# A tuned four-layer kernel: normalizing the early gates during the recurrence instead of in the gate stage

## The chip, the cores and the metric

The kernel runs on one core of one Trainium2 chip. The metric is the device time of one execution in microseconds (us). Several executions are timed and the median is given. One further execution is taken with the hardware profiler; every duration of a single instruction below comes from that one.

## The reference, cut to what matters

The input x has 16 sequences of 512 steps of 512 features. Four layers follow each other, each added to x. The change touches the third (L2) and the fourth (L3); the second (L1) sets the order in which everything can start.

```python
x = x + L0(x)                        # here: a gate per sequence and feature
# L1, a recurrence over the 512 steps
h = tanh(x_t @ Wx + b + h @ Wh);     x_t = x_t + h
# L2, over whole sequences, column by column of 512 features
f = sigmoid(x @ Wf.T + bf);  i = sigmoid(x @ Wi.T + bi);  c = x @ Wc.T + bc
s = f + i + 1e-8;  F = f / s;  I = i / s * c
scaling = exp(suffix sums of log(F + 1e-8))          # here: a product scan from the end
hidden  = cumsum(scaling * I) + exp(cumsum(log(F + 1e-8))) * h0
x = x + hidden
# L3, a matrix per sequence: base + low rank (rank 8), made from cond
layer = base + A_b @ B_b.T;          x = x + x @ layer
```

F and I of a step depend on that step alone, so they can be made as soon as L1 has finished the step. The scans need the whole sequence.

## The kernel before, in words

The program has two stages.

**The recurrence** (lines 399 to 478) goes through 64 blocks `n` of 8 steps `s`. Its instructions on TensorE, ScalarE, VectorE and SyncE stand in the order in which the source writes them (line 400). In each step TensorE does 16 matmuls of h with Wh (`accumulate`, L337, 32 instructions in the trace, since a matmul of this type is two instructions there), 8 matmuls of x with Wx for the next block (`inputs`, L337 too), and in part of the steps something else. ScalarE then does four tanh (L446) and VectorE four 32-wide transposes (L447), which give the h that the next step's matmuls wait for. After the transposes VectorE does one more operation in each step: the addition that makes L2's input x2 (L454, in steps 4 to 7 of a block, since the steps are added in pairs), or the gating of a later block's x (`gated`, L163, in steps 0 to 3).

Blocks 1 to 16 also make the low-rank factors of L3, in steps 4 to 7 of each block (`factor_part`, L309), in a PSUM bank with the tag `pf`.

**Early gates.** The weights of L2 are used on the first TE = 128 steps of every sequence already during the recurrence (`early_gate`, L379). One piece `q` is one k-chunk of one unit: 4 matmuls with 256 columns (2 sequences of 128 steps), put at the end of a recurrence step, while TensorE would otherwise wait for tanh and transposes. Four pieces make a unit: one of the three gates, for one of four 128-feature chunks `j`, for a pair of sequences. There are 8 pairs x 12 units x 4 = 384 pieces. They begin in block N_GATES = 17, one per step, and the last block does two per step. ScalarE takes each finished unit out of PSUM (`keep_gate`, L392: a sigmoid for f and i, the bias alone for the candidate), and SyncE's queue stores it in a DRAM tensor `early` with three parts (L393). Units alternate between two PSUM banks, `pf` and `pg`.

**The gate stage** (lines 481 to 589) goes through the 16 sequences `b`, and for each through 4 units `j` (`gate_unit`). A unit is 3 x 4 matmuls with the remaining 384 columns (L495) into `pf`, `pi` (one PSUM bank each) and `pc` (two banks), two sigmoids on ScalarE (L511), three loads of the early parts on SyncE's queue (L508 and L510), and eleven operations on VectorE: f + i + EPS (L512), the reciprocal of it (L513), f times it (L514), EPS added (L515), i times it (L516), i times the early candidate (L517, 128 columns), i times the new candidate straight from PSUM (L518), and three scans and a product (L522, L525, L526, L528). GpSimd adds the two parts (L531) and x2 (L532), which gives x3, L3's input. The tiles f, i and s have two buffers each, so a unit's sigmoid waits until GpSimd is done with the unit two before.

`make_layer` makes L3's matrix for sequence b after its unit j = 2: four matmuls (L553) into PSUM (`pl`, two in banks of its own and two in the banks of `po`), four copies on ScalarE (L559), and four additions of the base matrix on GpSimd (L560). For the last sequence VectorE adds into the base matrix itself (L557). `last_layer` of sequence b - 1 is done after unit j = 1 of sequence b: 16 matmuls with 512 columns (L567), evacuations on ScalarE (L571) and stores (L572). For the last sequence, b = 15, that `last_layer` of sequence 14 comes after j = 3, and its own follows as the last work of the program. In this stage a scheduler sets the order of each engine's instructions.

Of the kernel before, what the change touches and what calls it, by code (L numbers as in the profile page):

```python
# [30 lines left out]
F32 = mybir.dt.float32  # L31
# [4 lines left out]
P = 128  # L36
# [15 lines left out]


TE = 128
N_GATES = TE // T + 1
EPS = 1e-8
LN_EPS = 1e-5

# [5 lines left out]
def kernel(  # L64
# [27 lines left out]
    def col(which, j):  # L92
        return vec_sb[:, which * KC + j : which * KC + j + 1]
# [13 lines left out]
    base_sb = keep.tile([P, KC, D], F32)  # L107

    dram = ctx.enter_context(tc.tile_pool(name="dram", bufs=1, space=bass.MemoryType.DRAM))
    early = dram.tile([B, 3, KC, P, TE], F32, name="early")  # L110
    factor = [dram.tile([B, R, D], F32, name=f"factor_{i}") for i in range(2)]

    rnn = ExitStack()
# [253 lines left out]

    def early_gate(q):

        unit, k = divmod(q, KC)  # L370
        b, unit = divmod(unit, 3 * KC)
        which, j = divmod(unit, KC)
        pair = slice(2 * b, 2 * b + 2)
        if k == 0:
            pool, tag = ((ps_p, "pf"), (ps_q, "pg"))[unit % 2]
            early_gate.ps = pool.tile([P, 2, TE], F32, tag=tag, name=f"pg_{b}_{unit}")
        w = (wf_sb, wi_sb, wc_sb)[which]
        for c in range(KC):
            nc.tensor.matmul(  # L379
                early_gate.ps[c * BP : (c + 1) * BP, :, :],  # L380
                w[:, k, j * P + c * BP : j * P + (c + 1) * BP],
                x2[:, k, pair, :TE],
                start=(k == 0),
                stop=(k == KC - 1),
                skip_group_check=True,
            )
        return (pair, which, j, early_gate.ps) if k == KC - 1 else None

    def keep_gate(pair, which, j, ps):
        got = w2pool.tile([P, 2, TE], F32, tag="gate", name=f"gate_{pair.start}_{which}_{j}")  # L390
        func = AF.Identity if which == 2 else AF.Sigmoid
        nc.scalar.activation(got, ps, func, bias=col((C_BF, C_BI, C_BH)[which], j))  # L392
        nc.sync.dma_start(out=early[pair, which, j].rearrange("b p t -> p b t"), in_=got)  # L393

    def fresh(n):
        return [ps_r.tile([P, G, P], F32, tag=f"pre{i}", name=f"pre_{n}_{i}") for i in range(NBANK)]
# [8 lines left out]
    for n in range(NBLK):  # L405
        if n + 1 < NBLK:
            nxt = fresh(n + 1)
        if n + 2 < NBLK:
            xs.append(new_x1(n + 2))
        if n == 0:  # L410
            loaded = load_first()
        coming = None
        for s in range(T):
            odd = s % 2
            g = next(i for i, pair in enumerate(PAIRS) if s in pair)
            for k in range(KC):
# [12 lines left out]
            if loaded and s >= KC:  # L429
                factor_part(loaded, s - KC, *((straight, hT3) if n else (tile_columns, aeT)))  # L430
            made = []
            if n >= N_GATES:
                q = (n - N_GATES) * T + s
                qs = (q,) if n + 1 < NBLK else (q + s, q + s + 1)
                made = [gate for gate in map(early_gate, qs) if gate]
            a = apool.tile([P, P], F32, tag="a", name=f"a_{n}_{s}")

            h = h_out[s]
            if odd:
                turned, h_prev = h[:, :, :BP], h[:, :, B:]  # L440
            else:
                turned, h_prev = h[:, :, B:], h[:, :, :BP]
            bank, place = PLACE[g]
            for c in range(KC):
                at = slice(c * BP, (c + 1) * BP)
                nc.scalar.activation(a[:, at], pre[bank][:, place, at], AF.Tanh)  # L446
                nc.vector.transpose(turned[:, c, :], a[:, at])  # L447
            for gate in made:
                keep_gate(*gate)
            if s == max(PAIRS[g]):  # L450
                t0, t1 = PAIRS[g]
                step = t1 - t0
                at = slice(n * T + t0, n * T + t1 + step // abs(step), step)
                nc.vector.tensor_tensor(  # L454
                    x2[:, :, :, at].rearrange("p k b t -> p k t b"),
                    xs[n][:, :, t0 // 2, :, :],
                    turned.rearrange("p k (t b) -> p k t b", t=2),
                    ALU.add,
                )
# [30 lines left out]
    def gate_unit(b, j, x3):  # L490
        ps = []
        for w_sb, tag, bufs in ((wf_sb, "pf", 1), (wi_sb, "pi", 1), (wc_sb, "pc", 2)):
            p = ps_g.tile([P, S], F32, tag=tag, name=f"{tag}_{b}_{j}", bufs=bufs)
            for k in range(KC):
                nc.tensor.matmul(  # L495
                    p[:, TE:],
                    w_sb[:, k, j * P : (j + 1) * P],
                    x2[:, k, b, TE:],
                    start=(k == 0),
                    stop=(k == KC - 1),  # L500
                )
            ps.append(p)
        pf, pi, pc = ps
        f = work.tile([P, S], F32, tag="f", name=f"f_{b}_{j}")
        i = work.tile([P, S], F32, tag="i", name=f"i_{b}_{j}")
        s = work.tile([P, S], F32, tag="s", name=f"s_{b}_{j}")
        c = work.tile([P, TE], F32, tag="c", name=f"c_{b}_{j}")
        nc.sync.dma_start(out=c, in_=early[b, 2, j])  # L508
        for which, (gate, p, bias) in enumerate(((f, pf, C_BF), (i, pi, C_BI))):
            nc.sync.dma_start(out=gate[:, :TE], in_=early[b, which, j])  # L510
            nc.scalar.activation(gate[:, TE:], p[:, TE:], AF.Sigmoid, bias=col(bias, j))  # L511
        nc.vector.scalar_tensor_tensor(s, f, EPS, i, ALU.add, ALU.add)  # L512
        nc.vector.reciprocal(s, s)  # L513
# [4 lines left out]
        nc.vector.scalar_tensor_tensor(  # L518
            i[:, TE:], pc[:, TE:], col(C_BH, j), i[:, TE:], ALU.add, ALU.mult
        )  # L520
# [11 lines left out]
        nc.gpsimd.tensor_tensor(x3[:, j, :], s, x2[:, j, b, :], ALU.add)  # L532
# [13 lines left out]
    def make_layer(b, at, bt, layer):  # L546
# [6 lines left out]
            nc.tensor.matmul(pl, at[rows, :], bt[rows, :], start=True, stop=True)  # L553
            made.append(pl)
        for c, pl in enumerate(made):
            if layer is base_sb:
                nc.vector.tensor_tensor(layer[:, c, :], pl, layer[:, c, :], ALU.add)  # L557
# [90 lines left out]
```

## Time and profile before

| | us |
|---|---|
| median of 3 runs | 1698.56 |
| lowest and highest of them | 1697.42, 1702.98 |
| the profiled execution | 1701.3 |
| its span, first to last instruction | 1699.5 |
| TensorE busy | 1643.3 (97%) |
| VectorE busy | 1152.2 (68%) |
| ScalarE busy | 428.3 (25%) |
| GpSimd busy | 311.1 (18%) |
| recurrence ends, first matmul of the gate stage | 925.3 |
| last matmul of the gate stage issued and evacuated | 1696 |

The engines are PE (TensorE's matmuls; PEld are its weight loads), DVE (VectorE), ACT (ScalarE), POOL (GpSimd) and SP (SyncE). Times in the timeline are counted from the first instruction. A line of the timeline gives the start, the time taken, the engine, the source line, the operation, its output and inputs, and how many instructions were merged into it; in brackets stands the idle time before it and what ended that. A line of the groups gives the busy time and the mean duration in ns, then the idle time of the engine before such instructions. A line of the windows gives a stretch of time, then busy time and instruction count by engine, the granted TensorE clock, the busy share of the DMA engines and GB/s.

### The profile page before, as it was taken

How to read it: one execution, taken by the hardware profiler on the slowest of the kernel's cores; microseconds unless marked ns; L12 is line 12 of the kernel's file. 1: busy time of each engine (PE TensorE's matmuls, PEld its weight loads, DVE VectorE, ACT ScalarE, POOL GpSimd, SP SyncE). 2: the span in 40 equal slices, each digit the busy share in tenths (PEclk: the TensorE clock that was granted, in tenths of full speed). 3: DMA queues.
4: the chain of work that ended last, by engine and by line, in shares of the span. 5: the costliest groups of instructions: out<-in, count | busy, mean ns of one | idle time of the engine just before them, and what ended most of it. 6: DMA issues, size and time to landing. Idle time of an engine off the chain costs nothing.

```text
span 1699.5 us, 71490 instructions
## 1 busy us (share of the span) xinstructions
PE 1643.3 (97%) x31205; PEld 1197.7 (70%) x31205; DVE 1152.2 (68%) x3305; ACT 428.3 (25%) x2407; POOL 311.1 (18%) x283
## 2 busy tenths in 40 slices
PE   5999999999999999999999889999999999999987
PEld 5888888998999989998997445555555555555543
DVE  3444544444444444444443989999999999999994
ACT  2222223333333333333333111111121112212111
POOL 2000000000000000000000433334444444434331
PEclk9999999999999999999999999999999999999998
DMA  5344331111111111111111011011111111111101
GB/s 190 102 147 152 109 93 39 42 42 42 36 46 41 42 38 39 45 42 39 42 41 36 16 41 45 30 45 38 38 44 44 44 44 44 43 45 44 46 19 50
DMA packets 118160, 92.01 MB, mean 54 GB/s; under 512 B 11843, under 2 KB 96323, under 8 KB 117846
## 3 DMA queue, kind: packets, MB, share of 16 engines
q1 hardware_dynamic: 117312, 87.42, 16.8%
q8 instruction: 244, 4.00, 1.0%
q14 instruction: 70, 0.57, 0.1%
q10 hardware_dynamic: 534, 0.02, 0.0%
HBM read 57.51 MB, written 29.88 MB: 51 GB/s over the span
## 4 chain that ended last, share of the span: by engine, by line
PE 90%; DVE 6%; issue 1%; ACT 1%; DMA 1%; POOL 1%; DVEq 0%; ACTq 0%; POOLq 0%
PE pre L337 39%; PE po L567 13%; PE pg L379 10%; PE pf L495 9%; PE pi L495 8%; PE pc L495 8%; DVE s L513 2%; PE pf L309 1%; PE pl L553 1%; PE pre L355 1%; DVE h_out L447 1%; ACT a L446 1%; DVE s L522 1%; DVE s L526 1%; DMA b2a_raw<-in_b2a_dram 0%
## 5 line engine op out<-in xcount | busy, mean ns | idle before, releaser
L447 DVE STREAM_TRANSPOSE h_out<-a 128x32 f32<-128x32 f32 x2048 | 264.7, 186 | 454.5 <-ACT a L446 453.4
L337 PE MATMUL pre<-wh_sb,h_out 128*32 128x128 f32 x16384 | 560.4, 274 | 7.7 <-DVE h_out L447 1.4
L337 PEld LDWEIGHTS pre<-wh_sb,h_out 128*32 128x32 f32 x16384 | 460.8, 110 | 97.0 <-DVE h_out L447 71.9
L446 ACT ACTIVATE a<-pre 128x32 f32<-128x32 f32 x2048 | 238.3, 202 | 581.8 <-PE pre L337 581.7
L337 PE MATMUL pre<-wx_sb,x 128*32 128x128 f32 x8192 | 334.2, 273 | 2.4 <-issue 1.7
L337 PEld LDWEIGHTS pre<-wx_sb,x 128*32 128x32 f32 x8192 | 242.5, 110 | 5.0 <-issue 4.0
L567 PE MATMUL po<-layer,x 128*128 128x512 f32 x480 | 213.9, 604 | 14.2 <-DVE base_sb L557 9.8
L513 DVE RECIPROCAL s<-s 128x512 f32<-128x512 f32 x64 | 214.0, 3344 | 1.5
L495 PE MATMUL pf<-x,wf_sb 128*128 128x384 f32 x512 | 180.8, 497 | 11.4 <-ACT f L511 10.8
L567 PEld LDWEIGHTS po<-layer,x 128*128 128x128 f32 x480 | 93.0, 194 | 129.6 <-issue 106.5
L495 PE MATMUL pi<-x,wi_sb 128*128 128x384 f32 x512 | 175.8, 486 | 0.0
L495 PE MATMUL pc<-x,wc_sb 128*128 128x384 f32 x512 | 175.6, 486 | 0.0
L531 POOL TENSOR_TENSOR s<-s,f 128x512 f32<-128x512 f32 x64 | 93.7, 1464 | 429.0 <-DVE s L526 173.9
L484 POOL MEMSET zero<- 128x1 f32 x1 | 0.1, 99 | 911.6 <-DMA early<-gate 911.6
L495 PEld LDWEIGHTS pf<-x,wf_sb 128*128 128x128 f32 x512 | 96.9, 192 | 92.9 <-issue 19.9
L495 PEld LDWEIGHTS pi<-x,wi_sb 128*128 128x128 f32 x512 | 97.6, 191 | 68.3 <-issue 0.8
L495 PEld LDWEIGHTS pc<-x,wc_sb 128*128 128x128 f32 x512 | 97.3, 190 | 67.8
L454 DVE TENSOR_TENSOR x<-x,h_out 128x128 f32<-128x128 f32 x256 | 101.0, 395 | 34.9 <-PE pg L379 11.7
L511 ACT ACTIVATE f<-pf,vec_sb 128x384 f32<-128x384 f32 x64 | 37.3, 582 | 300.6 <-POOL s L531 279.9
L571 ACT COPY osb<-po 128x512 f32<-128x512 f32 x64 | 37.5, 586 | 233.4 <-DMA out_dram<-osb 125.2
L560 POOL TENSOR_TENSOR layer<-layer,base_sb 128x512 f32<-128x512 f32 x60 | 90.9, 1544 | 11.0 <-ACT layer L559 11.0
L379 PE MATMUL pg<-x,wf_sb 128*32 128x256 f32 x1024 | 84.6, 379 | 0.0
(84 smaller groups left out, 1334.2 us busy)
## 6 DMA issues: line engine op xcount, KB each, us to landing
xb<-in_xT_dram SPq DMA_DIRECT2D x64, 256.0 KB
w<-in_l3w_dram SPq DMA_DIRECT2D x64, 256.0 KB
out_dram<-osb SPq DMA_DIRECT2D x64, 256.0 KB
early<-gate SPq DMA_DIRECT2D x96, 128.0 KB
c<-early SPq DMA_DIRECT2D x64, 64.0 KB
f<-early SPq DMA_DIRECT2D x64, 64.0 KB
i<-early SPq DMA_DIRECT2D x64, 64.0 KB
w_sb<-in_w1T_dram SPq DMA_DIRECT2D x1, 1024.0 KB
```

The costliest lines, as they stand in the source:

```text
L337: nc.tensor.matmul(pre[PLACE[g][0]][j * BP : (j + 1) * BP, PLACE[g][1], :], lhsT, tile_columns(w, j), start=False, stop=False, skip_group_ ...
L379: nc.tensor.matmul(early_gate.ps[c * BP : (c + 1) * BP, :, :], w[:, k, j * P + c * BP : j * P + (c + 1) * BP], x2[:, k, pair, :TE], start= ...
L446: nc.scalar.activation(a[:, at], pre[bank][:, place, at], AF.Tanh)
L447: nc.vector.transpose(turned[:, c, :], a[:, at])
L454: nc.vector.tensor_tensor(x2[:, :, :, at].rearrange("p k b t -> p k t b"), xs[n][:, :, t0 // 2, :, :], turned.rearrange("p k (t b) -> p k ...
L495: nc.tensor.matmul(p[:, TE:], w_sb[:, k, j * P : (j + 1) * P], x2[:, k, b, TE:], start=(k == 0), stop=(k == KC - 1),)
L511: nc.scalar.activation(gate[:, TE:], p[:, TE:], AF.Sigmoid, bias=col(bias, j))
L513: nc.vector.reciprocal(s, s)
L531: nc.gpsimd.tensor_tensor(s, s, f, ALU.add)
L560: nc.gpsimd.tensor_tensor(layer[:, c, :], layer[:, c, :], base_sb[:, c, :], ALU.add)
L567: nc.tensor.matmul(po, x3[:, k, at], layer[:, k, :], start=(k == 0), stop=(k == KC - 1))
L571: nc.scalar.copy(osb, po)
```

## The change

The early gates are now normalized during the recurrence, and only the two finished tiles F and I (without the EPS that is added to F) are stored in `early`.

- `early_gate(q)` begins with step 128, that is in block 16, and there is one piece in every step to the last, so the doubled pieces of the last block are gone. The order of the units is changed, so that f, i and candidate of one (pair, j) follow each other: 12 pieces are a group.
- What was `keep_gate` becomes a list of jobs, each filed under the step in which it is to be issued (`later`, `do_jobs`). `do_jobs` stands at the end of a step, after its transposes and its addition or gating. Counted in steps from the group's first piece: sigmoid of f at 5, sigmoid of i at 7 (ScalarE); the sum f + i + EPS at 8; the reciprocal in four pieces of 64 columns at 9, 10, 11 and 12; f times it at 13, with the store; i times it at 14; and i times the candidate, straight from PSUM, at 15, with the store. So VectorE gets one job in eight of twelve steps. The tiles come from the pool of the L3 weights (`w2`, 6 buffers). Jobs left over after the last step are issued there.
- `gate_unit` does the sum, the reciprocal and both products on the 384 new columns alone. The loads of the early candidate (L508) and the product L517 are gone; the two other loads stay. The addition of EPS (L515), the scans and the products with them still take all 512 columns.
- `make_layer` adds the base matrix on VectorE, straight from PSUM, for every sequence; the ScalarE copies and the GpSimd additions are gone.

```diff
-N_GATES = TE // T + 1
...
-    early = dram.tile([B, 3, KC, P, TE], F32, name="early")
+    early = dram.tile([B, 2, KC, P, TE], F32, name="early")
...
     def early_gate(q):
-        unit, k = divmod(q, KC)
-        b, unit = divmod(unit, 3 * KC)
-        which, j = divmod(unit, KC)
+        u, k = divmod(q, KC)
+        group, which = divmod(u, 3)
+        b, j = divmod(group, KC)
...
-            pool, tag = ((ps_p, "pf"), (ps_q, "pg"))[unit % 2]
+            pool, tag = ((ps_p, "pf"), (ps_q, "pg"))[u % 2 if u else 1]
...
-    def keep_gate(pair, which, j, ps):
-        got = w2pool.tile([P, 2, TE], F32, tag="gate", name=f"gate_{pair.start}_{which}_{j}")
-        func = AF.Identity if which == 2 else AF.Sigmoid
-        nc.scalar.activation(got, ps, func, bias=col((C_BF, C_BI, C_BH)[which], j))
-        nc.sync.dma_start(out=early[pair, which, j].rearrange("b p t -> p b t"), in_=got)
...
+        def part_of_reciprocal(at):
+            nc.vector.reciprocal(flat[:, at], flat[:, at])
+        def normalize_f():
+            nc.vector.tensor_tensor(f, f, s, ALU.mult)
+            store(0, f)
+        def times_candidate():
+            nc.vector.scalar_tensor_tensor(i, ps, col(C_BH, j), i, ALU.add, ALU.mult)
+            store(1, i)
+        if which == 0:
+            later(q if u == 0 else q + 2, lambda: sigmoid(f, C_BF))
+        elif which == 1:
+            later(q, lambda: sigmoid(i, C_BI))
+            later(q + 1, lambda: nc.vector.scalar_tensor_tensor(s, f, EPS, i, ALU.add, ALU.add))
+            for n in range(4):
+                at = slice(n * TE // 2, (n + 1) * TE // 2)
+                later(q + 2 + n, lambda at=at: part_of_reciprocal(at))
+            later(q + 6, normalize_f)
+            later(q + 7, lambda: nc.vector.tensor_tensor(i, i, s, ALU.mult))
+        else:
+            later(q + 4, times_candidate)
+    jobs = {}
+    def later(q, job):
+        jobs.setdefault(q, []).append(job)
+    def do_jobs(q):
+        for job in jobs.pop(q, ()):
+            job()
...
-            made = []
-            if n >= N_GATES:
-                q = (n - N_GATES) * T + s
-                qs = (q,) if n + 1 < NBLK else (q + s, q + s + 1)
-                made = [gate for gate in map(early_gate, qs) if gate]
+            q = n * T + s - TE
+            if q >= 0:
+                early_gate(q)
...
-            for gate in made:
-                keep_gate(*gate)
...
+            do_jobs(q)
...
+    for q in sorted(jobs):
+        do_jobs(q)
     rnn.close()
...
-        c = work.tile([P, TE], F32, tag="c", name=f"c_{b}_{j}")
-        nc.sync.dma_start(out=c, in_=early[b, 2, j])
+        old, new = slice(0, TE), slice(TE, S)
...
-        nc.vector.scalar_tensor_tensor(s, f, EPS, i, ALU.add, ALU.add)
-        nc.vector.reciprocal(s, s)
-        nc.vector.tensor_tensor(f, f, s, ALU.mult)
+        nc.vector.scalar_tensor_tensor(s[:, new], f[:, new], EPS, i[:, new], ALU.add, ALU.add)
+        nc.vector.reciprocal(s[:, new], s[:, new])
+        nc.vector.tensor_tensor(f[:, new], f[:, new], s[:, new], ALU.mult)
         nc.vector.tensor_scalar(f, f, EPS, None, ALU.add)
-        nc.vector.tensor_tensor(i, i, s, ALU.mult)
-        nc.vector.tensor_tensor(i[:, :TE], i[:, :TE], c, ALU.mult)
+        nc.vector.tensor_tensor(i[:, new], i[:, new], s[:, new], ALU.mult)
...
-            if layer is base_sb:
-                nc.vector.tensor_tensor(layer[:, c, :], pl, layer[:, c, :], ALU.add)
-            else:
-                nc.scalar.copy(layer[:, c, :], pl)
-                nc.gpsimd.tensor_tensor(layer[:, c, :], layer[:, c, :], base_sb[:, c, :], ALU.add)
+            nc.vector.tensor_tensor(layer[:, c, :], pl, base_sb[:, c, :], ALU.add)
```

More of the change, by code (lines that the diff above doesn't have):

```diff
@@ L368, in early_gate @@
     def early_gate(q):
-        unit, k = divmod(q, KC)
-        b, unit = divmod(unit, 3 * KC)
-        which, j = divmod(unit, KC)
+        u, k = divmod(q, KC)
+        group, which = divmod(u, 3)
+        b, j = divmod(group, KC)
         pair = slice(2 * b, 2 * b + 2)
         if k == 0:
-            pool, tag = ((ps_p, "pf"), (ps_q, "pg"))[unit % 2]
-            early_gate.ps = pool.tile([P, 2, TE], F32, tag=tag, name=f"pg_{b}_{unit}")
+            pool, tag = ((ps_p, "pf"), (ps_q, "pg"))[u % 2 if u else 1]
+            early_gate.ps = pool.tile([P, 2, TE], F32, tag=tag, name=f"pg_{u}")
+        ps = early_gate.ps
         w = (wf_sb, wi_sb, wc_sb)[which]
@@ L379, in early_gate @@
             nc.tensor.matmul(
-                early_gate.ps[c * BP : (c + 1) * BP, :, :],
+                ps[c * BP : (c + 1) * BP, :, :],
                 w[:, k, j * P + c * BP : j * P + (c + 1) * BP],
@@ L386, in early_gate, with store, sigmoid @@
             )
-        return (pair, which, j, early_gate.ps) if k == KC - 1 else None
-    def keep_gate(pair, which, j, ps):
-        got = w2pool.tile([P, 2, TE], F32, tag="gate", name=f"gate_{pair.start}_{which}_{j}")
-        func = AF.Identity if which == 2 else AF.Sigmoid
-        nc.scalar.activation(got, ps, func, bias=col((C_BF, C_BI, C_BH)[which], j))
-        nc.sync.dma_start(out=early[pair, which, j].rearrange("b p t -> p b t"), in_=got)
+        if q % (3 * KC) == 0:
+            early_gate.tiles = [
+                w2pool.tile([P, D], F32, tag="w2", name=f"{name}_{group}", bufs=6)[:, : 2 * TE].rearrange(
+                    "p (b t) -> p b t", b=2
+                )
+                for name in ("ef", "ei", "es")
+            ]
+        if k < KC - 1:
+            return
+        f, i, s = early_gate.tiles
+        flat = s.rearrange("p b t -> p (b t)")
+        def store(which, got):
+            nc.sync.dma_start(out=early[pair, which, j].rearrange("b p t -> p b t"), in_=got)
+        def sigmoid(gate, bias):
+            nc.scalar.activation(gate, ps, AF.Sigmoid, bias=col(bias, j))
+        def part_of_reciprocal(at):
[24 more added lines that the diff above has]
+            job()
     def fresh(n):
@@ L506, in gate_unit @@
         s = work.tile([P, S], F32, tag="s", name=f"s_{b}_{j}")
-        c = work.tile([P, TE], F32, tag="c", name=f"c_{b}_{j}")
-        nc.sync.dma_start(out=c, in_=early[b, 2, j])
+        old, new = slice(0, TE), slice(TE, S)
         for which, (gate, p, bias) in enumerate(((f, pf, C_BF), (i, pi, C_BI))):
-            nc.sync.dma_start(out=gate[:, :TE], in_=early[b, which, j])
-            nc.scalar.activation(gate[:, TE:], p[:, TE:], AF.Sigmoid, bias=col(bias, j))
-        nc.vector.scalar_tensor_tensor(s, f, EPS, i, ALU.add, ALU.add)
-        nc.vector.reciprocal(s, s)
-        nc.vector.tensor_tensor(f, f, s, ALU.mult)
+            nc.sync.dma_start(out=gate[:, old], in_=early[b, which, j])
+            nc.scalar.activation(gate[:, new], p[:, new], AF.Sigmoid, bias=col(bias, j))
+        nc.vector.scalar_tensor_tensor(s[:, new], f[:, new], EPS, i[:, new], ALU.add, ALU.add)
+        nc.vector.reciprocal(s[:, new], s[:, new])
+        nc.vector.tensor_tensor(f[:, new], f[:, new], s[:, new], ALU.mult)
         nc.vector.tensor_scalar(f, f, EPS, None, ALU.add)
-        nc.vector.tensor_tensor(i, i, s, ALU.mult)
-        nc.vector.tensor_tensor(i[:, :TE], i[:, :TE], c, ALU.mult)
+        nc.vector.tensor_tensor(i[:, new], i[:, new], s[:, new], ALU.mult)
         nc.vector.scalar_tensor_tensor(
-            i[:, TE:], pc[:, TE:], col(C_BH, j), i[:, TE:], ALU.add, ALU.mult
+            i[:, new], pc[:, new], col(C_BH, j), i[:, new], ALU.add, ALU.mult
         )
```

## The prediction, as put on record before the changed kernel ran

> **What bounds the kernel now.** I read the windows first. Their columns are the stretch, its length, busy us and instructions of PE, PEld, DVE, ACT and POOL, the granted clock, the DMA share and GB/s.
>
> ```profile
> 930.00:1000.00 70.00, 57.69 (x162) 30.72 (x161) 64.26 (x59) 9.28 (x17) 23.71 (x21) 0.93 0.10 29
> 1100.00:1300.00 200.00, 200.00 (x600) 107.18 (x599) 198.52 (x189) 39.69 (x73) 86.25 (x71) 1.00 0.13 43
> 1600.00:1650.00 50.00, 47.10 (x148) 25.89 (x148) 49.62 (x51) 8.61 (x16) 19.84 (x17) 0.97 0.12 40
> 1650.00:1699.50 49.50, 36.10 (x81) 16.17 (x79) 26.58 (x30) 5.74 (x10) 7.92 (x6) 0.88 0.12 47
> ```
>
> In the middle of the gate stage PE and DVE are both full, so the shares don't say which sets the pace. The timeline of PE does:
>
> ```profile
> 951.68 2.85 PE L495 MATMUL pf<-x,wf_sb 128*128 128x384 f32 x8 [1.81 <-ACT f L511]
> 964.07 4.54 PE L495 MATMUL pf<-x,wf_sb 128*128 128x384 f32 x8 [4.37 <-ACT f L511]
> 990.47 9.88 PE L567 MATMUL po<-layer,x 128*128 128x512 f32 x17 [4.43 <-POOL x L532]
> ...
> 1166.42 2.74 PE L495 MATMUL pf<-x,wf_sb 128*128 128x384 f32 x8
> 1169.00 2.74 PE L495 MATMUL pi<-x,wi_sb 128*128 128x384 f32 x8
> 1171.58 2.74 PE L495 MATMUL pc<-x,wc_sb 128*128 128x384 f32 x8
> 1174.16 13.90 PE L567 MATMUL po<-layer,x 128*128 128x512 f32 x32
> ...
> 1635.23 2.85 PE L495 MATMUL pf<-x,wf_sb 128*128 128x384 f32 x8 [1.30 <-ACT f L511]
> 1645.91 4.35 PE L495 MATMUL pf<-x,wf_sb 128*128 128x384 f32 x8 [1.60 <-ACT f L511]
> 1665.42 16.75 PE L567 MATMUL po<-layer,x 128*128 128x512 f32 x32 [9.81 <-DVE base_sb L557]
> ```
>
> From 1004 to 1632 no PE line has a bracket: each group of 8 starts 2.58 us after the last (7.74 us a unit), the 32 of L567 take 13.74, and every sequence takes the same 45.96 us. So the middle is bound by PE's streaming; DVE's 45.6 us a sequence just fit. DVE binds only at the two ends. Start: streaming alone would bring sequence 2's first pf at 925.34 + 6 units (46.44) + L553's slot (1.25) + 13.74 = 986.8; it starts at 1004.05, so 17.3 us are lost. End: from 1601.55, 6 units, two L553 slots (2.3) and twice 13.74 would end at 1677.8; the last matmul ends near 1695.8, so 18.0 are lost.
>
> The recurrence, by DVE's timeline (ACT's tanh ends the .71 of idle time):
>
> ```profile
> 894.33 0.49 DVE L447 STREAM_TRANSPOSE h_out<-a 128x32 f32<-128x32 f32 x4 [0.71 <-ACT a L446]
> 895.03 0.40 DVE L454 TENSOR_TENSOR x<-x,h_out 128x128 f32<-128x128 f32 x1 [0.20 <-PE pg L379]
> 896.13 0.49 DVE L447 STREAM_TRANSPOSE h_out<-a 128x32 f32<-128x32 f32 x4 [0.71 <-ACT a L446]
> ```
>
> A step with an early gate takes 1.74 us or a little more, all of it PE issue: .87 for Wh, .44 for Wx, .43 for the gate. Steps without one take 1.645 (blocks 1 to 16); there PE waits for h. So the h chain has .095 us of slack under PE in a gate step, and DVE is free from 895.43 to 896.13.
>
> [...] L515 takes .42 alone and 1.48 at 951.49, beside L560. [...] behind 4.37 and 9.81 us of idleness the groups at 964.07 and 1665.42 take 1.8 and 2.85 us more; behind 1.60 it happened too (1645.91), behind 1.81 it didn't.
>
> **Part 1: a gate unit on DVE.** In the timeline L512 starts at 1208.33 and again at 1219.12: 10.79 us a unit away from L560. Rows used:
>
> ```profile
> L513 DVE RECIPROCAL s<-s 128x512 f32<-128x512 f32 x64 | 214.0, 3344 | 1.5
> L204 DVE RECIPROCAL rstd<-std 16x1 f32<-16x1 f32 x1 | 0.1, 150 | 2.1 <-ACT std L202 2.1
> L557 DVE TENSOR_TENSOR base_sb<-pl,base_sb 128x512 f32<-128x512 f32 x4 | 2.6, 660 | 0.0
> ```
>
> The reciprocal costs (3344 - 150) / 511 = 6.25 ns a column, so 128 columns less save .80. L512, L514 and L516 lose 128 columns at 1.04 ns (L516 .68 at 512 columns, L517 .28 at 128): .13 each, .40. L517 goes, .20 start to start, and .26 that L516 lay blocked in that unit. 10.79 - .80 - .40 - .20 - .26 = 9.13 us. Added: four base additions a sequence, some .60 each: 2.4 (for b = 15 they were there). [...] DVE's sequence falls from 45.6 to 4 x 9.13 + 2.4 = 38.9 us. In the middle that is worth nothing: 45.96 is PE's. ACT's copies and SP's 64 loads of c are off the path as well. GpSimd's L531 and L532 (2.6 us) begin as DVE starts the next unit's L512 and reciprocal, which they didn't slow at 1208.33; I take the same.
>
> **Part 2: the start.** Left-over jobs: one reciprocal piece (.47), two products (.42 each by the slope) and the candidate (.48) behind the last L454, 1.6 to 1.7 us. The first pf waited for the last reader of the early PSUM (ACT, 925.35); now that is DVE, so PE starts at 926.9. The last store lands some 2 us later (925.37 to 927.39 before). SP's queue then issues eight loads for L3 (.34 each, 927.31 to 930.06), and f's early part lands near 934.6. Before, L512 itself needed the early parts (it waited to 933.12); now the first that does is L515, 4.1 us into the unit. So DVE begins when pi is out: 926.9 + 5.16 + .6 = 932.7. Units end at 941.9, 951.0, 961.3 (with two base additions) and, after two more, 971.6; GpSimd gives x3 at 974.3. PE, never stopped by f's buffers on the way (the tightest, pf of unit 3, ends at 953.9, its buffer is free at 952.3), reaches L567 at 926.9 + 46.44 + 1.25 = 974.6, and first needs chunk 3 at 977.2. Sequence 2 starts at 988.3 against 1004.05: **15.7 us gained**. The cover is 2.9 us; each us of delay of DVE beyond it costs one. [...]
>
> **Part 3: the end.** L567 for sequence 14 waits for the third base addition of sequence 15. DVE is caught up at unit 2 of sequence 14 (pi out at 1607.3). Then, DVE-bound since nothing of L567 lies between: 1616.4, additions 1618.8, 1627.9, 1637.1, 1646.2, unit 2 of sequence 15 with two additions 1656.5, the third 1657.1. PE could be there at 1650.3. So L567 starts at 1657.1 instead of 1665.42, idle 6.8 instead of 9.81[...]. x3 of sequence 15 is ready at 1669.4, before 1673.7. **8.3 us gained.**
>
> **Part 4: the recurrence.** Block 16 gets 8 pieces. Its steps of 1.645 become 1.77 (14.15 us a block), and those with factor matmuls (8 instructions, .22) 1.99: 15.0 - 13.2 = 1.9 lost. The last block drops to one piece a step, so to the h chain's 1.645: 8 x .09 = .7 gained. Net **1.2 lost**. The jobs: 256 columns .42 to .48, a reciprocal piece 150 + 63 x 6.25 = 544 ns by the row, about .47 start to start. Behind L454 they start at 895.4 and end by 895.95, .2 before the next transposes; in steps with L163 there is more room. What waits behind a job is the next transposes, and for them PE, with .095 of cover more. I take 0; a longer job is bounded below under the rivals. The candidate's bank is needed again at the next step's gate, .2 us after the job. SP's stores fall from 96 to 64.
>
> **Sum.** 1699.5 - 15.7 - 8.3 + 1.2 = 1676.7 of span; the profiled execution took 1.8 more than its span and lay 2.7 over the median, so 1678.5 there. The median: 1698.56 - 22.8 = **1676** us.
>
> **Rivals.** *Only part of the start is regained*[...]: PE lost 4.4 at 964 and 4.4 at 990 to such waits. If half of the 15.7 stays lost: 1684. For it: the 2.9 us of cover is thin. *All PE idleness goes*: 17.3 + 18.0 instead of 15.7 + 8.3, so 1665; against it, six units without L567 between need 7.74 of PE and 9.13 of DVE each. *The jobs lie in the h chain*, the slower case: a job behind L454 that outlasts the free time delays transposes, then PE. Half of the 256 jobs stand there. Free are .70 and the .095: .8 us. To be slower by 5 us the 24 us of gain must be eaten too, 28 / 128 = .22 us each, so jobs of 1.0 us where I reckon .42 to .54. At 1.05 us: 1708. Below zero such a job can't go, since nothing is removed from those steps' chain. *Nothing happens* would need DVE to stay the limit at both ends: no row supports it.
>
> **Chances.** Forecast (1671 to 1681) .60, part of the start .20, all idleness .10, jobs in the chain .10, of which .06 end slower and .03 near no change. A difference of .3% (5 us) is what the measurement can tell. Faster .91, same .03, slower .06. The range takes in the second and third case in part: 1667 to 1687.
>
> **What would show it.** Right: first L567 without a bracket near 975, sequences still 45.96 us apart, L567 of sequence 14 near 1657 on this span's clock, L513's mean near 2.54 us, gate steps still 1.74. Wrong: gate steps of 1.8 or more with PE waiting for h_out; PE brackets between 975 and 990; a period other than 45.96.

## The result and the profile after

| | before | after |
|---|---|---|
| median of 4 runs each, us | 1699.24 | 1677.82 |
| lowest and highest | 1697.42, 1702.98 | 1675.61, 1679.41 |
| profiled execution | 1701.3 | 1677.59 |
| its span | 1699.5 | 1675.8 |
| TensorE busy | 1643.3 | 1638.2 |
| VectorE busy | 1152.2 | 1126.2 |
| GpSimd busy | 311.1 | 213.4 |

The ratio is 0.987, with a 95% interval of 0.985 to 0.9891: 21.4 us less. Lines of the changed file have other numbers: the gate matmuls are L541, the sigmoids L556, sum and reciprocal of a unit L557 and L558, the last scan L570, GpSimd's additions L575 and L576, the base addition L600, the last layer's matmuls L607 with copies L611 and stores L612. In the recurrence L491 is tanh, L492 the transposes, L497 the addition behind them, L410 a piece of the reciprocal, L413, L429 and L417 the three products.

The windows of after, with the columns of those of before (PE, PEld, DVE, ACT, POOL, clock, DMA share, GB/s):

```profile
930.00:1000.00 70.00, 69.81 (x212) 37.70 (x211) 59.92 (x66) 9.77 (x18) 20.70 (x21) 1.00 0.11 34
1100.00:1300.00 200.00, 200.00 (x593) 107.24 (x592) 169.82 (x196) 29.87 (x52) 54.77 (x52) 1.00 0.10 34
1630.00:1675.80 45.80, 35.81 (x80) 15.82 (x78) 21.11 (x25) 5.74 (x10) 8.02 (x6) 0.88 0.13 49
```

At the start PE went from 57.69 of 70 us to 69.81. In the middle DVE fell from 198.52 of 200 us to 169.82, and PE is as full as it was. At the end PE still lacks 10 us. The timeline of PE shows where:

```profile
925.64 2.82 PE L541 MATMUL pf<-x,wf_sb 128*128 128x384 f32 x8 [0.98 <-DVE x L497]
...
973.42 13.90 PE L607 MATMUL po<-layer,x 128*128 128x512 f32 x32
987.15 2.74 PE L541 MATMUL pf<-x,wf_sb 128*128 128x384 f32 x8
...
996.31 1.12 PE L597 MATMUL pl<-bt,at 8*128 8x512 f32 x2 [0.19 <-ACT osb L611]
...
1112.61 13.90 PE L607 MATMUL po<-layer,x 128*128 128x512 f32 x32
...
1158.57 13.90 PE L607 MATMUL po<-layer,x 128*128 128x512 f32 x32
...
1585.96 2.74 PE L541 MATMUL pf<-x,wf_sb 128*128 128x384 f32 x8
...
1641.44 16.98 PE L607 MATMUL po<-layer,x 128*128 128x512 f32 x32 [6.34 <-DVE base_sb L600]
1658.26 13.90 PE L607 MATMUL po<-base_sb,x 128*128 128x512 f32 x32
```

Read it in four stretches, each against before. The first gate matmul comes at 925.64 instead of 925.34: +0.3. From there to the second pf of this list, behind the first L607, are 61.5 us instead of 78.7: -17.2, all of the 17.3 that the prediction found lost there. (The prediction calls this pf sequence 2's first. Six units lie ahead of it, four of sequence 0 and two of sequence 1, so it is unit 2 of sequence 1.) From it to unit 2 of sequence 14 (1585.96; 1601.55 before) are 598.8 instead of 597.5: +1.3, one new wait, at 996.31; elsewhere the sequences are 45.96 apart (1158.57 less 1112.61), as before. The bracket shows .19 of that wait alone, since the record of the matmuls ahead of it is drawn out (1.13 us for six at 994.99, where eight take 1.14 at 949.02): the next pf comes at 997.36, 5.05 behind the pc at 992.31, where in the next sequence it comes 3.74 behind. From 1585.96 to the end of the span are 89.8 instead of 97.95: -8.1. The sum is -23.7, the difference of the two spans.

### The profile page after: what moved, and what is told of

Same layout as the page of the kernel before. It is cut to its first block, busy times and chain, and to the rows that moved or that the text cites. A ratio compares the mean times of both kernels' runs of the same rounds, so it can differ in the third digit from the quotient of the medians.

```text
span 1675.8 us, 71396 instructions
## 1 busy us (share of the span) xinstructions
PE 1638.2 (98%) x31205; PEld 1196.9 (71%) x31205; DVE 1126.2 (67%) x3557; ACT 381.6 (23%) x2315; POOL 213.4 (13%) x223
## 4 chain that ended last, share of the span: by engine, by line
PE 89%; DVE 6%; issue 2%; DMA 1%; ACT 1%; POOL 0%; ACTq 0%; SPq 0%; DVEq 0%; POOLq 0%
PE pre L336 40%; PE po L607 12%; PE pg L382 10%; PE pf L541 8%; PE pi L541 8%; PE pc L541 8%; DVE s L558 2%; PE pf L308 1%; PE pl L597 1%; DVE s L566 1%; PE pre L354 1%; DVE h_out L492 1%; DVE s L570 1%; ACT a L491 1%; DMA b2a_raw<-in_b2a_dram 0%
## 5 line engine op out<-in xcount | busy, mean ns | idle before, releaser
L336 PEld LDWEIGHTS pre<-wh_sb,h_out 128*32 128x32 f32 x16384 | 462.1, 110 | 97.0 <-DVE h_out L492 71.1
L492 DVE STREAM_TRANSPOSE h_out<-a 128x32 f32<-128x32 f32 x2048 | 262.0, 185 | 364.1 <-ACT a L491 363.5
L491 ACT ACTIVATE a<-pre 128x32 f32<-128x32 f32 x2048 | 238.3, 202 | 627.0 <-PE pre L336 626.8
L607 PE MATMUL po<-layer,x 128*128 128x512 f32 x480 | 211.5, 599 | 6.3 <-DVE base_sb L600 6.3
L541 PE MATMUL pf<-x,wf_sb 128*128 128x384 f32 x512 | 177.3, 489 | 1.0 <-DVE x L497 1.0
L607 PEld LDWEIGHTS po<-layer,x 128*128 128x128 f32 x480 | 92.2, 192 | 120.2 <-issue 108.8
L541 PE MATMUL pi<-x,wi_sb 128*128 128x384 f32 x512 | 175.6, 486 | 0.0
L541 PE MATMUL pc<-x,wc_sb 128*128 128x384 f32 x512 | 175.6, 486 | 0.0
L558 DVE RECIPROCAL s<-s 128x384 f32<-128x384 f32 x64 | 163.4, 2553 | 2.2
L541 PEld LDWEIGHTS pf<-x,wf_sb 128*128 128x128 f32 x512 | 95.9, 190 | 79.9 <-issue 18.1
L541 PEld LDWEIGHTS pc<-x,wc_sb 128*128 128x128 f32 x512 | 97.3, 190 | 67.8
L541 PEld LDWEIGHTS pi<-x,wi_sb 128*128 128x128 f32 x512 | 97.3, 190 | 67.8
L575 POOL TENSOR_TENSOR s<-s,f 128x512 f32<-128x512 f32 x64 | 87.5, 1367 | 388.8 <-DVE s L570 376.2
L497 DVE TENSOR_TENSOR x<-x,h_out 128x128 f32<-128x128 f32 x256 | 101.1, 395 | 37.5 <-PE pg L382 13.8
L557 DVE SCALAR_TENSOR_TENSOR s<-f,i 128x384 f32<-128x384 f32 x64 | 36.6, 572 | 101.7 <-ACT i L556 101.7
L556 ACT ACTIVATE f<-pf,vec_sb 128x384 f32<-128x384 f32 x64 | 37.3, 583 | 276.1 <-POOL s L575 117.3
L611 ACT COPY osb<-po 128x512 f32<-128x512 f32 x64 | 37.5, 586 | 273.7 <-PE po L607 159.5
L382 PE MATMUL pg<-x,wc_sb 128*32 128x256 f32 x1024 | 84.0, 379 | 0.0
```

The costliest lines, as they stand in the source:

```text
L336: nc.tensor.matmul(pre[PLACE[g][0]][j * BP : (j + 1) * BP, PLACE[g][1], :], lhsT, tile_columns(w, j), start=False, stop=False, skip_group_ ...
L382: nc.tensor.matmul(ps[c * BP : (c + 1) * BP, :, :], w[:, k, j * P + c * BP : j * P + (c + 1) * BP], x2[:, k, pair, :TE], start=(k == 0), s ...
L497: nc.vector.tensor_tensor(x2[:, :, :, at].rearrange("p k b t -> p k t b"), xs[n][:, :, t0 // 2, :, :], turned.rearrange("p k (t b) -> p k ...
L541: nc.tensor.matmul(p[:, TE:], w_sb[:, k, j * P : (j + 1) * P], x2[:, k, b, TE:], start=(k == 0), stop=(k == KC - 1),)
L556: nc.scalar.activation(gate[:, new], p[:, new], AF.Sigmoid, bias=col(bias, j))
L557: nc.vector.scalar_tensor_tensor(s[:, new], f[:, new], EPS, i[:, new], ALU.add, ALU.add)
```

## The experiments

Three groups of runs were made, each beside its own runs of before (medians 1701.60, 1701.02 and 1699.90), so ratios are compared, and times only within a group. The theory: VectorE's shorter unit removes the stops at the start, its earlier base additions part of the stop at the end, the middle is PE's, and the jobs lie free behind the transposes. The main rival: the gain comes from taking away GpSimd's base addition alone, beside which VectorE's operations take longer in before (L514 1.32 us at 1198.04, beside the L560 of 1197.55, and .69 alone at 1212.42); then `e1_base_only` would take about 1680 us and `e2_gates_only` about 1694.

### Each part alone

`e1_base_only` is before with the base added by VectorE; the gates are as they were.

```diff
-                nc.scalar.copy(layer[:, c, :], pl)
-                nc.gpsimd.tensor_tensor(layer[:, c, :], layer[:, c, :], base_sb[:, c, :], ALU.add)
+                nc.vector.tensor_tensor(layer[:, c, :], pl, base_sb[:, c, :], ALU.add)
```

> The kernel before, with the base matrix of L3 added by VectorE alone; early gates as before. If the gain of the whole change came from DVE being the limit at the two ends of the gate stage only: near the start the L560 additions blocked DVE for 5.8 us between 949 and 960 and four additions of .6 replace them, so 3.4 us less; near the end 3.8 against 2.4, so 1.4 less; the middle stays at 45.96 us a sequence. About 1694 us, of 1699. [...] If VectorE was the limit throughout the stage: 16 x (3.5 - 2.4) = 18 us less, about 1682, with a shorter period.

Measured: 1699.35, ratio 0.9982 (0.9973 to 0.999), a gain of 2.3 us. PE's timeline still has the stops of before:

```profile
952.63 4.54 PE L495 MATMUL pf<-x,wf_sb 128*128 128x384 f32 x8 [1.81 <-ACT f L511]
...
972.57 4.17 PE L495 MATMUL pf<-x,wf_sb 128*128 128x384 f32 x8 [2.50 <-ACT f L511]
...
989.30 13.95 PE L563 MATMUL po<-layer,x 128*128 128x512 f32 x26 [4.45 <-POOL x L532]
...
1664.07 17.06 PE L563 MATMUL po<-layer,x 128*128 128x512 f32 x32 [11.51 <-DVE base_sb L556]
```

The rival falls, and the 5 us that I gave this part were too many. The timeline of DVE in the same run says why:

```profile
950.76 1.75 DVE L516 TENSOR_TENSOR i<-i,s 128x512 f32<-128x512 f32 x1
952.44 1.48 DVE L515 TENSOR_SCALAR f<-f 128x512 f32<-128x512 f32 x1
```

These two take .68 and .42 alone. Beside them lie GpSimd's additions of the unit before (1.47 at 950.49 and 1.59 at 952.04 in this run). They lay there in before too, as its timelines of DVE and POOL show:

```profile
949.55 1.47 POOL L531 TENSOR_TENSOR s<-s,f 128x512 f32<-128x512 f32 x1 [18.19 <-DVE s L526]
949.81 1.75 DVE L516 TENSOR_TENSOR i<-i,s 128x512 f32<-128x512 f32 x1
951.10 1.60 POOL L532 TENSOR_TENSOR x<-s,x 128x512 f32<-128x512 f32 x1
951.49 1.49 DVE L515 TENSOR_SCALAR f<-f 128x512 f32<-128x512 f32 x1
952.65 6.55 POOL L560 TENSOR_TENSOR layer<-layer,base_sb 128x512 f32<-128x512 f32 x4
```

So of the 5.8 us that DVE lost between 949 and 960, 2.1 were due to L531 and L532 (1.75 less .68, and 1.49 less .42), and only the 3.7 of the four slow operations behind them to L560. The expectation put all of it down to L560, against which stand four base additions of .6 on DVE. In both an operation of VectorE lies beside one of GpSimd and takes longer: L515 1.49 us beside L532, L517 1.35 at 952.90 beside L560, against .42 and .28 alone. What the two engines share there is not shown. Taking away one GpSimd neighbour leaves the other: L516 and L515 still take 1.75 and 1.48 here. In this run unit 2 of sequence 1 comes 76.8 us behind the first gate matmul (78.7 in before); from unit 2 of sequence 14 to the end of the span nothing is gained (97.9 in both).

`e2_gates_only` is after with the base added as before.

```diff
-            nc.vector.tensor_tensor(layer[:, c, :], pl, base_sb[:, c, :], ALU.add)
+            if layer is base_sb:
+                nc.vector.tensor_tensor(layer[:, c, :], pl, layer[:, c, :], ALU.add)
+            else:
+                nc.scalar.copy(layer[:, c, :], pl)
+                nc.gpsimd.tensor_tensor(layer[:, c, :], layer[:, c, :], base_sb[:, c, :], ALU.add)
```

> The changed kernel with the base added as before (ScalarE copies, GpSimd adds). If DVE's work at the two ends is what pays: the start has 1.5 us of cover and loses 5.8 - 2.4 - 1.5 = 1.9 us or none where the blocked operations differ, the end loses 1.4: about 1681 us against 1678. [...]

Measured: 1682.78, ratio 0.9895 (0.988 to 0.991), a gain of 18.8. The start has no stop, as in after. The last stop begins the same way and is longer:

```profile
1645.27 17.06 PE L611 MATMUL po<-layer,x 128*128 128x512 f32 x32 [8.94 <-DVE base_sb L601]
```

That is 718.4 us behind this run's first gate matmul (926.89), against 715.8 in after. So the gates bring 18.8 and the base 2.3 alone, 21.1 together; the whole change brought 21.4 in its own runs and 24.0 in the repetition below. The parts add up within what runs scatter; whether the base is worth more once the gates are light can't be told from these runs. Most of the gain is the gates'.

### Is it VectorE's load?

`e5_more_vector` is after with VectorE given back about the load that the change took: a reciprocal of 256 columns more per unit, whose result nobody uses.

```diff
+        spare = work.tile([P, 2 * TE], F32, tag="spare", name=f"spare_{b}_{j}", bufs=1)
+        nc.vector.reciprocal(spare, s[:, TE : 3 * TE])
```

> The changed kernel with one more reciprocal of 256 columns a unit, into a tile that nobody reads: 150 + 255 x 6.25 = 1744 ns, some 1.7 us start to start, so DVE's sequence is 45.6 us again as in the kernel before. If DVE binds only at the ends: four units of it before the first L607 (6.8, less 1.5 of cover) and five between sequence 14's unit 2 and sequence 15's base additions (8.4): 5.3 + 8.4 = 13.7 us more, about 1691.5[...]; sequences still 45.96 us apart. If DVE's total is the limit: 64 x 1.7 = 109 us more, about 1787. If DVE is off the path everywhere: 1678.

Measured: 1696.89, ratio 0.9973 (0.9965 to 0.9981). Of the 1.3 to 1.4% that the change brings elsewhere, 0.27% is left, less than I expected. The window and PE's timeline:

```profile
1100.00:1300.00 200.00, 199.74 (x593) 107.02 (x592) 198.25 (x210) 29.81 (x52) 56.45 (x54) 1.00 0.11 35
```

```profile
969.42 2.85 PE L541 MATMUL pf<-x,wf_sb 128*128 128x384 f32 x8 [2.44 <-ACT f L556]
975.80 2.85 PE L541 MATMUL pc<-x,wc_sb 128*128 128x384 f32 x8 [0.95 <-DVE i L564]
984.11 13.12 PE L609 MATMUL po<-layer,x 128*128 128x512 f32 x26 [2.88 <-POOL x L578]
...
1662.61 16.59 PE L609 MATMUL po<-layer,x 128*128 128x512 f32 x32 [12.09 <-DVE base_sb L602]
```

DVE's load in the middle is before's (198.25 against 198.52), and PE is still at 199.74: 28 us of work per 200 moved little there. It was not nothing. From unit 2 of sequence 1 to unit 2 of sequence 14 are 600.2 us, 2.7 more than in before, since from the sixth sequence on most take 46.15 to 46.44 and not 45.96, with short waits of PE. The 109 us of a DVE that limits everywhere are out. Unit 2 of sequence 1 comes 70.3 us behind the first gate matmul (61.5 in after, 78.7 before), and the last stop comes 65.3 behind unit 2 of sequence 14 (55.5 in after). So the load decides at the two ends, as predicted, with 8.8 and 9.8 us where 5.3 and 8.4 were expected.

At the start 8.4 us of the gain stayed in spite of the load. The traces show what else differs there. In before DVE begins 7.8 us behind the first gate matmul, since its sum waits for an early part; in this run it begins 6.05 behind. And in before the sum and the reciprocal of unit 1 stand ahead of the last scans of unit 0:

```profile
939.13 0.69 DVE L512 SCALAR_TENSOR_TENSOR s<-f,i 128x512 f32<-128x512 f32 x1 [1.93 <-ACT i L511]
943.14 3.33 DVE L513 RECIPROCAL s<-s 128x512 f32<-128x512 f32 x1
948.12 1.20 DVE L526 TENSOR_TENSOR_SCAN s<-i,zero 128x512 f32<-128x512 f32 x1
```

So unit 0 ended 24.0 us behind the first gate matmul, and GpSimd could free the buffers for unit 2 only then; here it ended 17.5 behind, in after 15.7. Last, of the 5.8 us that DVE lost beside GpSimd in before about 1 is left here. No run separates these three.

### How long may a job be?

`e8_after_again` is after unchanged, beside the next two. `e3_two_pieces` has the reciprocal in two pieces of 128 columns, `e4_one_piece` in one of 256 (the diff is that of e4; e3 has `range(2)` and pieces of `TE` columns at `q + 2` and `q + 4`).

```diff
-            for n in range(4):
-                at = slice(n * TE // 2, (n + 1) * TE // 2)
-                later(q + 2 + n, lambda at=at: part_of_reciprocal(at))
+            later(q + 2, lambda: part_of_reciprocal(slice(0, 2 * TE)))
```

> The changed kernel as it is, on the chip of the three others, so that they can be set against it: 0.987 of the kernel before, some 1679 us where that takes 1701.

> The changed kernel with the reciprocal of the early gates in two pieces of 128 columns (150 + 127 x 6.25 = 944 ns by the slope) in place of four of 64. In the trace of the changed kernel a job behind the addition starts .83 us before the next transposes in a step of 1.645 us, so .92 in a step of 1.74, and .095 of cover come on top: 1.02 us. If that is the room, 944 ns fit and nothing changes: 0.987. If the room was as short as I had reckoned (.8): 32 such jobs behind an addition x .14 = 4.5 us more.

> The same in one piece of 256 columns (1.74 us, about 1.68 start to start). If the jobs lie in the h chain as soon as they outlast the room: behind the addition (16 of 32) 1.68 - 1.02 = .66 late, behind the gating, which ends earlier, 1.68 - 1.23 = .45 late, 16 x (.66 + .45) = 18 us more, about 1696 where the changed kernel takes 1678, with PE waiting for h_out. If the jobs are off the chain whatever they take: 1678.

Measured: 1677.03 (0.9862, 0.9847 to 0.9878), 1676.53 (0.9858, 0.9844 to 0.9873) and 1691.21 (0.9944, 0.9932 to 0.9957). A piece takes 536 ns in after, 936 in e3, 1736 in e4. First the room, in DVE's timeline of after:

```profile
520.56 0.49 DVE L492 STREAM_TRANSPOSE h_out<-a 128x32 f32<-128x32 f32 x4 [0.52 <-ACT a L491]
521.20 0.40 DVE L497 TENSOR_TENSOR x<-x,h_out 128x128 f32<-128x128 f32 x1
521.43 0.53 DVE L410 RECIPROCAL es<-es 128x64 f32<-128x64 f32 x1
522.31 0.49 DVE L492 STREAM_TRANSPOSE h_out<-a 128x32 f32<-128x32 f32 x4 [0.35 <-ACT a L491]
```

The job ends .35 before the next transposes can start, so they wait for tanh and not for it. From its start to the transposes are .88; with the .095 that PE covers, .98. The expectation had 1.02 from another step. The 936 ns of e3 still fit. In e4 they don't:

```profile
502.24 1.73 DVE L410 RECIPROCAL es<-es 128x256 f32<-128x256 f32 x1
503.88 0.42 DVE L490 STREAM_TRANSPOSE h_out<-a 128x32 f32<-128x32 f32 x4
504.41 0.39 DVE L495 TENSOR_TENSOR x<-x,h_out 128x128 f32<-128x128 f32 x1
505.47 0.49 DVE L490 STREAM_TRANSPOSE h_out<-a 128x32 f32<-128x32 f32 x4 [0.67 <-ACT a L489]
```

The transposes at 503.88 have lost their bracket: they wait for DVE itself. They come 2.51 behind those at 501.37 in that trace, a regular step being 1.74 or 1.75. The next come 1.59 later, so .15 is caught up, and .6 is lost. In half of the steps the job stands behind L162, which is shorter, and there is more room: a step of 2.24 instead of 2.51. The first gate matmul of e4 is at 939.42 instead of 925.95. The 14.2 us over e8 are .44 for each of the 32 long jobs, less than the .56 that I expected. The slower rival of the prediction is thus a real mechanism, and its threshold lies between .94 and 1.74 us.

### Other things that the change moved

`e9_extra_loads` is after with a third load of an early part for each unit, as before the change, into a tile that nothing reads.

```diff
+        c = work.tile([P, TE], F32, tag="c", name=f"c_{b}_{j}")
+        nc.sync.dma_start(out=c, in_=early[b, 1, j])
```

> The changed kernel with a third early load a unit put back (64 KB, into a tile that nobody reads), so that SyncE issues as many loads in the gate stage as before. If the loads were only off the path: 0.986 to 0.987 of the kernel before, as the changed kernel. If fewer loads on SyncE's queue were part of the gain, as the 4 x .47 us that they take ahead of the first units' f and i and the wait of L597 in sequence 1 suggest: some us more, at most 0.99.

Measured: 1678.12, ratio 0.9866 (0.9849 to 0.9884), as e8 within the intervals. So 64 more loads on SyncE's queue cost nothing that these runs can tell. Nothing waits for the tile here; in before L517 needed it, and that need e9 does not bring back.

### What is left at the end, and the new wait

`e6_split_last` is after with the last layer of sequence 14 cut in two: its tiles 0 and 1 go in behind unit 2 of sequence 15, tiles 2 and 3 behind unit 3. PE then has something to do while DVE catches up.

```diff
-            if j == (KC - 1 if end else 1) and pending is not None:
+            if end and j == 2:
+                last_layer(*pending, tiles=range(2))
+            elif end and j == 3:
+                last_layer(*pending, tiles=range(2, 4))
+            elif not end and j == 1 and pending is not None:
```

> The changed kernel with sequence 14's last matmuls in two halves, two tiles behind unit 2 of sequence 15 and two behind unit 3. If the 6.3 us of waiting and the slow matmuls behind it (3.1 us) are what DVE's lag over six units in a row costs: the third base addition is then due 6.9 us later on PE, the wait goes, and PE waits only some 2.8 us for the last unit's x3[...]: about 1671 to 1674. If the end is bound by something else: 1678.

> Sequence 14's last matmuls in two halves once more, SyncE issuing the output stores, on the chip of the next one: 0.985.

Measured: 1674.52, ratio 0.9849 (0.9831 to 0.9866), and in the repetition (e10, the same kernel) 1674.34, ratio 0.9856 (0.9841 to 0.987). The intervals overlap with those of after, so the medians don't tell what the split alone is worth. In the traces it is 3.1 to 4.6 us: from unit 2 of sequence 14 to the end of the span are 85.3 (e6) and 85.2 (e10), in after and e8 89.8 and 88.4. The stop behind L600 is gone; a shorter one for x3 of the last sequence remains, again with a slow group behind it (26 matmuls take 11.3 us at the rate of 13.90 for 32):

```profile
1656.26 13.10 PE L607 MATMUL po<-base_sb,x 128*128 128x512 f32 x26 [2.30 <-POOL x L576]
```

The new wait at 996.31 in after leads from PE to ScalarE's fourth copy of the layer output:

```profile
995.67 0.59 ACT L611 COPY osb<-po 128x512 f32<-128x512 f32 x1 [10.29 <-DMA out_dram<-osb]
```

It waited 10.29 us for the buffer of an earlier store. SyncE's queue tells why the store was late:

```profile
989.75 0.32 SPq L555 DMA_DIRECT2D i<-early  x1
991.09 0.32 SPq L555 DMA_DIRECT2D f<-early  x1
991.46 5.15 SPq L612 DMA_DIRECT2D out_dram<-osb  x3
```

The stores stand behind loads of unit 3, and those wait until VectorE (up to 7.0 us for L570, between 975 and 1000) and GpSimd (up to 1.2 us for L575) free their tiles. To test it, `e7_split_act_store` is e6 with these stores on ScalarE's queue; e11 repeats it beside e10.

```diff
-            nc.sync.dma_start(out=out[b, at, :], in_=osb)
+            nc.scalar.dma_start(out=out[b, at, :], in_=osb)
```

> The kernel with sequence 14's last matmuls in two halves, and the stores of the output issued by ScalarE instead of SyncE. If the wait of L597 for an evacuation in sequence 1 (1.3 us) comes from output stores queued on SyncE behind loads of f and i that wait for their buffers: the bracket goes, 1.3 us less than with SyncE's stores, about 0.984 of the kernel before. If it comes from the transfers themselves: no change, 0.985.

> The same with ScalarE issuing the output stores. The first time it took 3.9 us less than the other on another chip, 1.3 of it the wait of L597, some 3 in the recurrence, where both have the same instructions. If that was scatter: 1.3 us less than the run beside it. If it comes with the program: some 4 us less, and the recurrence ends near 922.6 again instead of 925.7.

Measured: 1670.56, ratio 0.9826 (0.9811 to 0.9841), and 1671.53, ratio 0.9835 (0.982 to 0.985), in e11. In PE's timeline the four products of sequence 1 run through:

```profile
997.83 1.14 PE L597 MATMUL pl<-bt,at 8*128 8x512 f32 x8
```

In e10 the same eight take 2.06 (at 996.80). So the wait came from the order on the queue; removing it is worth .9 in the traces of e10 and e11. In the eight profiles with PE on time there and the stores on SyncE's queue, sequence 1 takes .5 to 1.3 us more than 45.96 (in e6 3.0, with a slow group behind the wait); in the two with ScalarE's it takes 45.96. The medians differ by 2.8 (e10 and e11). Of the rest, 1.7 of the profiled runs is the group behind the last stop, which took 11.43 in e11 and 13.12 in e10 behind equal idleness (2.35 and 2.31). This doesn't come with the edit, since it took 13.12 in e7 too. The recurrence of e7's profile ended 3 us earlier than e6's, that of e11 1 us later than e10's: scatter too. With both edits the kernel is the fastest of all, 6.5 us under after in the same group (e8).

## Why the prediction was right, step by step

**The start** was the largest term, 15.7 us, less 1.2 for the recurrence ahead of it: 14.5. Measured are 16.9 to the same point. The chain was the right one: DVE's units, predicted to end at 941.9, 951.0, 961.3 and 971.6, ended at 941.3, 950.4, 961.0 and 971.5; x3 was ready at 974.6 (974.3 predicted), and L607 began without a bracket:

```profile
940.13 1.20 DVE L570 TENSOR_TENSOR_SCAN s<-i,zero 128x512 f32<-128x512 f32 x1
973.30 1.27 POOL L576 TENSOR_TENSOR x<-s,x 128x512 f32<-128x512 f32 x1
```

The step that was mis-sized is "now that is DVE, so PE starts at 926.9", 1.6 us for the left-over jobs. They do lie there, to 927.6, but PE waited for L497 alone: its first gate matmul comes 1.12 behind the start of the last transposes (924.52), in before 1.16 behind (924.18). The bank whose reader is the last job is not the one that the first unit fills. So the 1.6 were nothing; the rest of the 2.4 lies in the recurrence. PE came earlier than reckoned and DVE hardly, so the cover of DVE, called thin at 2.9, was some 1.4 us by the same count (chunk 3 needed at 976.0). It held. That it was there owes something to the order: the prediction took the units one after another, without a reason, where the kernel before had unit 1's sum and reciprocal within unit 0. The order came as taken, which was luck.

**A gate unit** was predicted at 9.13 us, and is 9.13 from start to start (971.38 to 980.51); a sequence of DVE 38.9, and 169.82 of 200 us are 39.0. The slope drawn from two reciprocals gave 2.54 and .544 us for the two new sizes:

```profile
L558 DVE RECIPROCAL s<-s 128x384 f32<-128x384 f32 x64 | 163.4, 2553 | 2.2
L410 DVE RECIPROCAL es<-es 128x64 f32<-128x64 f32 x128 | 68.5, 536 | 0.0
```

One reading of VectorE beside GpSimd was wrong, though no sum rests on it: the L515 at 951.49 lies beside L532 and not L560 (see `e1_base_only`). The four additions of L560 take 6.03 us at 1197.55 in before, and DVE loses 3.8 there (L514 to L517 take 5.9 instead of 2.1).

**The middle at nothing** was right for DVE and wrong by 1.3 us for one sequence. "ACT's copies and SP's 64 loads of c are off the path as well" looked at what was removed. It did not look at what stands behind what on SP's queue once PE runs on time: the output stores of the first last layer, behind loads that wait for tiles. e7 and e11 show that cause.

**The end**: predicted 8.3, measured 8.1. L607 was put 55.55 us behind unit 2 of sequence 14 (1657.1 less 1601.55), and came 55.48 behind it. A slow group behind the stop was in the sum (1673.7 less 1657.1 are 16.6); it took 16.98, where 32 take 13.90 elsewhere.

**The recurrence**: block 16 was to lose 1.9 and lost 2.05 (13.16 to 15.21); steps of the last block fell to 1.645 as said; blocks with gates stayed at 14.15. At its end the net 1.2 can't be told from chance: in ten profiles with this recurrence (four or two pieces) the first gate matmul lies between 922.63 and 929.10, mean 926.4; in the two with the old one it lies at 925.34 and 926.29. From the transposes of step 128, where the edit begins, to those of the last step the ten take 680.1 us on average (678.4 to 681.1), the two 679.3 and 678.8: 1.0 more, near the 1.2, though single profiles scatter as much. The jobs cost nothing that shows: PE's weight loads waited 71.1 us for h in all, against 71.9 before. The room for a job was "some .8"; measured is about 1.0. The .70 was counted from the end of L454 in the records; but a job starts .23 us after the start of that addition (521.43 against 521.20), which is .17 before its recorded end.

**The rivals.** *Only part of the start* is out: all of it came back, and in e5, with 1.7 us more a unit, 8.8 of it went again. *All PE idleness* is out at the end, where 6.34 us of idleness and the slow group (16.98 instead of 13.90) remain; e6 shows that it needs another order. *Jobs in the h chain* is out at .54 us and comes true at 1.74 (e4).

## What to carry to other kernels

An engine that is full beside another full one may not matter in the steady state and still set both ends, where the other engine has no other work to do while it catches up. So price a lighter VectorE by the stops at the ends and not by its busy time: 28 us of work per 200 were worth 2.7 us over the whole middle, and 18.6 at the ends. Work could be put into this chain of short steps at no cost that shows while each piece (up to .94 us) fitted into the free time behind the critical instruction; cut it to that size, and measure the size. Before you blame one GpSimd instruction for a slow one on VectorE, look in the trace which one stands beside it: L515 still took 1.48 us with L560 gone. When a stall goes, look then at each queue on which a store stands behind a load that waits for a tile.

## What the runs showed of the hardware that was not expected

- **A group of matmuls behind a stop can be slow, and by no fixed amount.** Behind the same 6.34 us of idleness the 32 matmuls took 16.98 (after), 15.60 (e8), 15.59 (e3) and 17.02 us (e4), instead of 13.90: 1.7 to 3.1 us more. The granted clock (the third number from the end) agrees; of after and then of e8:

```profile
1643.00:1645.00 2.00, 2.00 (x3) 0.67 (x2) 2.00 (x1) 0.00 (x0) 0.69 (x1) 0.50 0.00 0
1645.00:1647.00 2.00, 2.00 (x4) 0.95 (x3) 1.97 (x6) 0.00 (x0) 0.00 (x0) 0.50 0.00 0
1645.00:1647.00 2.00, 2.00 (x6) 0.95 (x5) 1.97 (x5) 0.03 (x1) 0.00 (x0) 1.00 0.00 0
```

Shorter stops can cost it too, and not each time. Behind 2.3 us it happened in e6, e7 and e10 (13.10 to 13.12 us for 26 matmuls) and not in e11 (11.43); behind 1.81 us in e1 (the pf at 952.63 took 4.54) and not in before (951.68, 2.85); and behind the new wait of some 1.2 us in e6 alone, where the pf at 997.46 took 4.53 instead of 2.85. What decides it is not shown.
- **A piece of a VectorE reciprocal costs the same slope at each size**: 536, 936, 1736, 2553 and 3344 ns at 64, 128, 256, 384 and 512 columns, 6.25 ns a column and some .14 us on top. Cutting 256 columns in four costs .4 us more of DVE each time.
- **Single recurrence steps of 2 to 3 us** turn up in every trace, some of them at the same step again (the step from 230 to 231 takes 2.1 to 2.8 us in five of the ten profiles); the profile names only PE's issue ahead of them. The end of the recurrence moves by up to 6.5 us between the ten profiles, and 5.3 of it stand already at step 128 (243.2 to 248.4 us). The cause stays open.
